# Regrouped loads, one fold for the attention biases, and a longer waking matmul in a three-layer attention kernel

## The chip, the cores and the metric

The kernel runs on one core of one Trainium2 chip. The metric is the device time in microseconds of one launch. The engines are TensorE (PE in the profile, with its weight loads as PEld), VectorE (DVE), ScalarE (ACT), GpSimd (POOL) and SyncE (SP), which in this kernel issues nearly all DMAs.

## The reference

A batch of 16 sequences of 256 tokens with 256 features (`x`), and a context `y` of the same size. All numbers are float32. There are 16 heads of 16 features.

```python
# layer 0: cross-attention with RMS norms
q, c = rmsnorm(x, g_q), rmsnorm(y, g_c)
x = rmsnorm(x + softmax((q @ Wq) (c @ Wk)^T / 4) (c @ Wv) @ Wo, g_out)
# layer 1: causal self-attention, with biases and rotary positions
h = ln1(x);  x = x + attn(rope(h @ sa_wq + b), rope(h @ sa_wk + b), h @ sa_wv + b, causal) @ sa_wo + b
# layer 2: cross-attention with the context
h = ln2(x);  x = x + attn(rope(h @ ca_wq + b), rope(y @ ca_wk + b), y @ ca_wv + b) @ ca_wo + b
# then an MLP
h = ln3(x);  out = x + gelu(h @ fc1_w + fc1_b) @ fc2_w + fc2_b
```

Each layer norm has a gain `g` and a bias `b`. The kernel never applies them to the tokens. It multiplies the gain into the rows of the weight that follows (`fold_gain`), and computes `b @ W` once with a few small matmuls, to add it to the bias of that product ("a fold").

## The kernel before, in words

The 48 attentions (3 layers x 16 batches) run one after the other in the order that the string `ORDER` gives (line 31): 0 is layer 0, 1 the causal self-attention, 2 the second cross-attention. One pass of the loop over `i` is called slot `i` here, and takes some 13 to 15 us. The first slots are of layers 0 0 0 0 0 1 0 1 0 1 0 2 2 1 0 2. The MLP of all batches follows, in seven-product form (`Mlp`), from 727 us on.

The order of instructions on each engine is written out by hand (`manual_schedule`): every engine takes its instructions in the order in which the Python calls are made. A slot has 4 steps `n` (3 in a causal slot). Each step issues the scores of one block (L484, PE), their exponentials (L495, ACT), in causal slots the mask (L502, POOL), and the product with the values of the step before (L523, PE); in between, PE works for the neighbours: `q`, `k` (L286) and `v` (L299) of attention i+1, the output projection (`project`, L299) of i-2, and the transpose of the normed tokens (`turn`, L266) of i+2.

An attention's result passes through DRAM. The copy of `av` out of PSUM (L540) is written to `hop` (L541). `end`, at step 0 of the next slot, writes the second half and reads back the softmax sums (`sums`, L548) and the rows (`oT`, L553). `invert`, at step 1, takes the reciprocal (L560), writes it to `inv_hop` (L562) and reads it back spread over the partitions (`inv`, L568). `divide` multiplies both (L574) a slot later. For layer 0, `send` and `receive` take the norm's factor the same way, through `rq_hop` (L363) to `rq` (L371).

Loads of inputs: each attention of layer 0 needs its batch's x and y in two layouts, rows (`x`, `y`) and transposed (`xT`, `yT`), 256 KB each. Batches 0 to 3 are loaded before the loop, batch 4 in slot 0. From slot 2 on, a slot whose attention i+3 is of layer 0 (a load slot: 3, 5, 7, 11 and so on, 11 of them) calls `load` at its start, ahead of all its other DMAs: xT, x, yT, y. The weights of the later layers (`pieces`: three of `ca`, `cao`, four of `fc1`, four of `fc2`, 256 KB each) are issued one each at the end of steps 1 and 2 of the slots after 3 in which attention i+3 is not of layer 0. All go through SP's queue, in which `hop`, `sums`, `oT`, `inv` and `rq` stand too.

Folds: `fold_v` (L207) adds the layer norm's share to V's bias row of self-attention, at slot 0, step 3, with PE products and a DVE addition that waits for `bias_sb`. `fold_bias` makes the products for Q and K in one row each and writes them to DRAM (`fold_hop`); `fold_back` (L186) reads them back as columns, in 4-byte pieces. For self-attention these are at slots 1 and 2, the addition (`fold_sa`, L195) at slot 3. For cross-attention they are at slot 6, step 3 (products) and slot 8, step 2, where the read (`fold_back`), `fold_gain` and the addition (`fold_ca`, L198) are called together. For fc1 they are at slot 11 and at slot 14, step 2, where read and addition (`fold_fc1`, L202) are again called together.

The start: two matmuls on a tile of zeros (`idle`, L878, of 512 and 256 columns) run while the first loads are under way. `stats` (L238) computes the sums of squares on DVE, POOL takes the power (L231, into `pad` and `r_o`), and `spread` (L350, PE) spreads the factor of the first two batches.

Of the kernel before, what the change touches and what calls it, by code (L numbers as in the profile page):

```python
# [12 lines left out]
ALU = mybir.AluOpType  # L13
# [32 lines left out]
def xattn_kernel(  # L46
# [27 lines left out]
    def ctile(shape, name, dtype=F32):  # L74
        return const.tile(shape, dtype, tag=name, name=name)
# [8 lines left out]
    def rows_of(b):  # L84
        return cur[:, NC * b : NC * b + NC, :]
# [3 lines left out]
    xTs = {}  # L89
    yTs = {}  # L90

    def load_x(b):
        xTs[b] = work.tile([P, KC, S], F32, tag="xT", name=f"xT{b}", bufs=3)
        nc.sync.dma_start(out=xTs[b], in_=xt[b].rearrange("(k p) s -> p k s", p=P))
        nc.sync.dma_start(out=rows_of(b), in_=x[b].rearrange("(c p) d -> p c d", p=P))

    def load_y(b):
        yTs[b] = work.tile([P, KC, S], F32, tag="yT", name=f"yT{b}", bufs=Y_LIVE)
        nc.sync.dma_start(out=yTs[b], in_=yt[b].rearrange("(k p) s -> p k s", p=P))
        ys[b] = work.tile([P, NC, D], F32, tag="y", name=f"y{b}", bufs=3)  # L100
        nc.sync.dma_start(out=ys[b], in_=y[b].rearrange("(c p) d -> p c d", p=P))

    def load(b):
        load_x(b)
        load_y(b)

    def load_w(t, aps, eng):
        at = 0
# [7 lines left out]
    nc.scalar.dma_start(out=vec, in_=vecs)  # L116
    w0_sb = ctile([P, KC, 3 * D], "w0")
    load_w(w0_sb[:, :, : 2 * D], w0[:2], nc.scalar)
    load_x(0)
    load_y(0)  # L120
    mask_u8 = ctile([P, B * NC], "mask_u8", U8)
    w0o_sb = ctile([P, KC, D], "w0o")
    sa_sb = ctile([P, KC, 3 * D], "sa")
# [27 lines left out]
    def dense_ps():  # L151
        return psD.tile([P, 512], F32, tag="d", name="d")
# [38 lines left out]

    qk_cols = vec[:, V_QK : V_QK + 8].rearrange("p (n t) -> p n t", t=KC)

    def fold_sa(cols):
        nc.vector.tensor_tensor(qk_bias[:, 0:2], cols[:, 0:2], qk_cols[:, 0:2], ALU.add)  # L195

    def fold_ca(cols):
        nc.vector.tensor_tensor(qk_bias[:, 2], cols[:, 0], qk_cols[:, 2], ALU.add)  # L198
        nc.vector.tensor_copy(qk_bias[:, 3], qk_cols[:, 3])

    def fold_fc1(cols):
        nc.vector.tensor_tensor(  # L202
            fb1.rearrange("p (j t) -> p j t", t=KC), cols,
            vec[:, V_FC1B : V_FC1B + FF // P].rearrange("p (j t) -> p j t", t=KC), ALU.add,
        )

    def fold_v():  # L207
        ps = dense_ps()
        for k in range(KC):
            for j in range(0, P, 32):  # L210
                nc.tensor.matmul(
                    ps[j : j + 32, :D],
                    lhsT=vec[:, V_B1 + k : V_B1 + k + 1].to_broadcast([P, 32]),
                    rhs=sa_sb[:, k, 2 * D : 3 * D],
                    start=(k == 0), stop=(k == KC - 1), skip_group_check=True,
                )
        row = bias_sb[:, R_SAV : R_SAV + D]
        nc.vector.tensor_tensor(row, ps[:, :D], row, ALU.add)

    def fold_gain(w, cols, vcol, chunks=range(KC), eng=nc.vector):  # L220
        for k in chunks:
# [652 lines left out]
    with tc.manual_schedule():  # L874

        idle = psS.tile([P, 2, 512], F32, tag="S", name="idle")[:, 0]
        for n in (512, 256):
            nc.tensor.matmul(idle[:, :n], lhsT=ident, rhs=zeros[:, :n], start=True, stop=True)  # L878
        fold_gain(w0_sb, slice(0, D), V_GQ)

# [23 lines left out]
        pieces = [(ca_sb[:, :, j * D : (j + 1) * D], [ca[j]], nc.sync) for j in range(3)]  # L904
        pieces.append((cao_sb, [ca_o], nc.sync))
        for j in range(4):
            cols = slice(j * D, (j + 1) * D)
            pieces.append((fc1_sb[:, :, cols], [fc1[:, cols]], nc.sync))
        for j in range(4):
            pieces.append((fc2_sb[:, 2 * j : 2 * j + 2], [fc2[j * D : (j + 1) * D]], nc.sync))  # L910
        for i in range(N_ATT):
            a, last = att(i), att(i - 1)
            ahead = att(i + 3)
            if i > 1 and ahead is not None and ahead.layer == 0:
                load(ahead.b)

# [7 lines left out]
            for n in range(len(a.blocks)):  # L924
                if n == 0 and a.causal and not finishing:
                    do(i + 2, "stats")
                a.scores(n)
                if n > 0:
                    a.values(n - 1)
                elif last is not None:  # L930
                    last.values(-1)
                final = len(a.blocks) - 1
                if n == 0:
                    if i == 0:
                        a.v()
# [12 lines left out]
                    if i == N_ATT - 3:  # L948
                        mlps[0].stats()
                    if i == N_ATT - 2:  # L950
                        mlps[0].norm()
                    do(i - 2, "divide")
                    if i == N_ATT - 1:
                        mlps[0].turn(nc.vector.tensor_copy)
                        mlps[0].keep()
                    do(i + 1, "q")
                elif n == 1:

                    if a.causal:
# [12 lines left out]
                    if i == N_ATT - 1:  # L972
                        do(i - 2, "project")
                        mlps[1].norm()
                if n == final - 1:
                    do(i + 1, "v")
                    if i == N_ATT - 2:
                        mlps[1].stats()
                    if i == N_ATT - 1:
                        mlps[0].up(2)  # L980
                        mlps[0].mix("hT")
                if n == final:
                    if i == N_ATT - 1:
# [530 lines left out]
```

## Time and profile before

| | |
|---|---|
| Median of 3 runs | 949.86 us (947.06, 949.86, 951.55) |
| Profiled execution, its own time | 948.64 us |
| Its span, first to last instruction | 946.9 us |
| Mean granted TensorE clock | 0.997 |
| DVE busy | 664.8 us (70%) |
| ACT busy | 547.0 us (58%) |
| POOL busy | 310.6 us (33%) |
| DMA, SP's queue | 80.58 MB, 27.0% of 16 engines' span |

PE is busy for nearly all of the span, so a mean says little here: it has to be asked where PE stands, and behind what. The view of windows gives PE's busy time in stretches of 20 us; the timeline of a short stretch shows each engine's instructions in order of time and, in brackets, how long the engine stood before one and what released it. The ends of matmuls are modelled, so a wait can hide in a busy PE: a group of matmuls that starts late after the one before is then seen only by comparing start times with those of the same group elsewhere.

Two landmarks for the timeline: slot 5 begins at 89.41, slot 6 at 103.50, slot 8 at 133.35, slot 9 at 148.91, slot 14 at 228.49 and slot 15 at 244.63 us.

### The profile page before, as it was taken

The numbers are of one execution on the slowest core, as the hardware profiler recorded it, in microseconds if no ns is written. First come the engines' busy times: TensorE is split into PE (matmuls) and PEld (weight loads), VectorE is DVE, ScalarE is ACT, GpSimd is POOL, SyncE is SP. The second block draws the span as 40 slices with busy tenths as digits, with TensorE's granted clock in tenths as the row PEclk, the third lists the DMA queues.
The fourth block names the chain that finished last, engine by engine and source line by source line (L and its number), as shares of the span: only waits on it lengthen the run. The fifth ranks groups of instructions, "written<-read, shape, count | busy, mean of one in ns | idle before, by whom it ended". The sixth has DMA issues, their size and how long they took to land.

```text
span 946.9 us, 29342 instructions
## 1 busy us (share of the span) xinstructions
PE 934.5 (99%) x12390; PEld 551.1 (58%) x12390; DVE 664.8 (70%) x1439; ACT 547.0 (58%) x773; POOL 310.6 (33%) x503
## 2 busy tenths in 40 slices
PE   8999998999999999999999999999999999999997
PEld 4444454445454555455455454555444799999997
DVE  4457765776777778768876677988877576676663
ACT  3666654765656665756656666666666634444440
POOL 4213452315352554434443333454133021222200
PEclk9999999999999999999999999999999999999999
DMA  9443343524242232322434221222222100000001
GB/s 293 139 118 107 110 157 86 165 70 145 64 128 87 73 125 87 115 78 71 126 110 133 87 90 62 80 68 71 77 72 81 46 23 24 12 12 24 23 24 47
DMA packets 99893, 83.07 MB, mean 88 GB/s; under 512 B 22686, under 2 KB 99498, under 8 KB 99754
## 3 DMA queue, kind: packets, MB, share of 16 engines
q1 hardware_dynamic: 99066, 80.58, 27.0%
q8 instruction: 99, 1.62, 0.7%
q10 hardware_dynamic: 688, 0.54, 0.2%
q14 instruction: 40, 0.33, 0.1%
HBM read 50.92 MB, written 30.17 MB: 86 GB/s over the span
## 4 chain that ended last, share of the span: by engine, by line
PE 91%; DMA 4%; DVE 2%; SPq 1%; issue 1%; POOL 0%; ACT 0%; ACTq 0%; DVEq 0%
PE S L484 18%; PE A L523 17%; PE d L286 16%; PE d L299 16%; PE upX L688 6%; PE A L786 5%; PE downZ L786 3%; PE upZ L688 3%; PE d L266 2%; PE d L786 2%; PE d L688 1%; DMA hop<-av 1%; DMA cols<-fold_hop 1%; PE d L664 1%; PE downX L786 1%
## 5 line engine op out<-in xcount | busy, mean ns | idle before, releaser
L495 ACT ACTIVATE pt<-S 128x1024 f32<-128x1024 f32 x224 | 217.3, 1022 | 119.9 <-PE S L484 119.7
L484 PE MATMUL S<-qm,kT 32*128 32x512 f32 (+1 forms) x1536 | 201.8, 600 | 0.0
L523 PE MATMUL A<-pt,va 128*32 128x256 f32 (+1 forms) x3072 | 190.4, 368 | 3.5 <-POOL pt L502 2.5
L523 PEld LDWEIGHTS A<-pt,va 128*32 128x32 f32 x3072 | 80.4, 109 | 157.9 <-issue 106.8
L495 ACT ACTIVATE pt<-S,sy 128x1024 f32<-128x1024 f32 x128 | 135.6, 1111 | 46.4 <-PE S L484 45.9
L502 POOL TENSOR_SCALAR_AFFINE_SELECT pt<-pt 128x512 f32<-128x512 f32 x128 | 88.8, 709 | 62.5 <-ACT pt L495 62.2
L484 PEld LDWEIGHTS S<-qm,kT 32*128 32x128 f32 x1536 | 62.3, 183 | 65.3 <-issue 41.2
L275 POOL TENSOR_TENSOR cur<-cur,bias 128x512 f32<-128x512 f32 x48 | 66.5, 1391 | 56.5 <-DVE xn L255 56.5
L230 POOL TENSOR_SCALAR r_ln<-bmv 128x2 f32<-128x2 f32 x48 | 14.1, 295 | 214.7 <-DVE bmv L249 213.5
L394 ACT ACTIVATE a<-d,qk_bias 128x256 f32<-128x256 f32 x128 | 53.6, 470 | 52.4 <-PE d L286 40.9
L286 PE MATMUL d<-hT,sa 128*32 128x256 f32 x1024 | 61.1, 379 | 0.0
L583 DVE TENSOR_TENSOR cur<-d,cur 128x512 f32<-128x512 f32 x32 | 22.0, 687 | 44.7 <-PE d L299 44.7
L255 DVE TENSOR_SCALAR xn<-cur,bmv,r_ln 128x256 f32<-128x256 f32 x96 | 52.1, 591 | 1.4 <-POOL r_ln L231 0.8
L540 DVE COPY av<-A 128x512 f32<-128x512 f32 x47 | 32.4, 688 | 26.6 <-PE A L523 25.6
L402 DVE TENSOR_TENSOR u<-u,turn 128x512 f32<-128x512 f32 x64 | 49.7, 777 | 0.0
L402 DVE TENSOR_TENSOR a<-a,turn 128x512 f32<-128x512 f32 x64 | 47.2, 737 | 2.2
L398 DVE STREAM_SHUFFLE u<-a 128x512 f32<-128x512 f32 x64 | 47.5, 742 | 0.0
L726 ACT ACTIVATE g<-g,fb 128x256 f32<-128x256 f32 x96 | 41.0, 499 | 11.1 <-DVE g L715 11.1
L230 POOL TENSOR_SCALAR r_o<-ms_o 128x2 f32<-128x2 f32 x16 | 3.8, 240 | 132.0 <-DVE sq L238 122.4
L286 PEld LDWEIGHTS d<-hT,sa 128*32 128x32 f32 x1024 | 33.5, 110 | 21.8
L574 DVE TENSOR_TENSOR oT<-oT,inv 128x512 f32<-128x512 f32 x48 | 42.6, 889 | 3.2 <-issue 2.5
L781 DVE TENSOR_TENSOR g<-g,g 128x512 f32<-128x512 f32 x64 | 40.9, 681 | 0.0
(152 smaller groups left out, 1572.1 us busy)
## 6 DMA issues: line engine op xcount, KB each, us to landing
hop<-av SPq DMA_DIRECT2D x96, 256.0 KB
oT<-hop SPq DMA_DIRECT2D x96, 128.0 KB
inv<-inv_hop SPq DMA_DIRECT2D x96, 128.0 KB
xT<-in_xt SPq DMA_DIRECT2D x16, 256.0 KB
cur<-in_x SPq DMA_DIRECT2D x16, 256.0 KB
yT<-in_yt SPq DMA_DIRECT2D x16, 256.0 KB
y<-in_y SPq DMA_DIRECT2D x16, 256.0 KB
out<-res SPq DMA_DIRECT2D x15, 256.0 KB
```

The lines of the kernel that those rows point to most:

```text
L255: nc.vector.tensor_scalar(xn[:, c, :], src[:, c, :], mv[:, c, 0:1], r[:, c : c + 1], ALU.subtract, ALU.mult,)
L275: nc.gpsimd.tensor_tensor(t, t, bias_sb[:, row : row + D].unsqueeze(1).to_broadcast([P, NC, D]), ALU.add)
L286: nc.tensor.matmul(ps[j : j + 32, t * S : (t + 1) * S], lhsT=w[:, k, at + t * P + j : at + t * P + j + 32], rhs=src[:, k, :], start=(k == ...
L299: nc.tensor.matmul(ps[j : j + 32, c * D : (c + 1) * D], lhsT=src[:, k, c * P + j : c * P + j + 32], rhs=w[:, k, at : at + D], start=(k == ...
L394: nc.scalar.activation(a[:, t], ps[:, t], AF.Identity, bias=bias[:, t : t + 1])
L402: nc.vector.tensor_tensor(t, t, table.unsqueeze(1).to_broadcast([P, KC, S]), ALU.mult)
L484: nc.tensor.matmul(ps[:, j, 2 * m * u : 2 * m * (u + 1)] .rearrange("p (i s) -> p i s", i=2), lhsT=self.kT[r, t, kc * P : (kc + 1) * P], r ...
L495: nc.scalar.activation(pt[:, :, :w], ps[:, :, :w], AF.Exp, scale=scale)
L502: nc.gpsimd.affine_select(out=diag, in_=diag, compare_op=ALU.is_ge, fill=0.0, base=0, pattern=[[0, 2], [0, 2], [1, P]], channel_multiplier=-1,
L523: nc.tensor.matmul(self.av[32 * r : 32 * r + 32, i, q0:S], lhsT=self.va[:, kc, 8 * t + 2 * r + i, :], rhs=pts[r // 2][:, r % 2, i * m : (i ...
L688: nc.tensor.matmul(banks[c // 2][:, (c % 2) * S : (c % 2 + 1) * S], lhsT=a[:, c * P : (c + 1) * P], rhs=b, start=(first and c % 2 == 0), s ...
L786: nc.tensor.matmul(ps[:, c, :], lhsT=a[f // 2][:, f % 2, c * P : (c + 1) * P], rhs=b[:, f, :], start=(first and c == 0 and f == 0), stop=True,
```

## The change

- Loads of the loop: `batch` makes the list of a batch's four loads, in the order x, y, xT, yT. In a load slot the four are put at the head of a list `due`, in which the later weights (without Wq of cross-attention) already wait. `load_next(i)` issues from the list at two places of a slot: at step 0 behind `end`, and at step 1 behind `invert` and `receive`. In a load slot it issues two each time, else one each time from slot 3 on.
- Before the loop and in slot 0, batches 1 to 4 are loaded in the order x, y, xT, yT; batch 0 keeps xT, x, yT, y.
- Wq of cross-attention is loaded at slot 0, step 1, instead of slot 4.
- Folds: one call at slot 1, step 3 makes the products for Q, K and V of self-attention and Q of cross-attention. Slot 2 reads the columns back, and the V row, spread over all partitions, into a new tile `row_v`. `fold_att` at slot 3, step 3 makes all additions. `fold_v`, the call of `fold_bias` at slot 6 and the addition at slot 8 are gone; `fold_gain` at slot 8 stays.
- fc1's fold is read back at slot 12, step 1, and added at slot 14, step 2 as before.
- The second waking matmul has 384 columns instead of 256.

```diff
+    def load(b, order=(0, 1, 2, 3)):
+        pieces = batch(b)
+        for n in order:
+            nc.sync.dma_start(out=pieces[n][0], in_=pieces[n][1])
...
-    load_x(0)
-    load_y(0)
+    load(0, (2, 0, 3, 1))
...
+    def fold_att(cols, row_v):
+        for n, j in ((0, 0), (1, 1), (2, 3)):
+            nc.vector.tensor_tensor(qk_bias[:, n], cols[:, j], qk_cols[:, n], ALU.add)
         nc.vector.tensor_copy(qk_bias[:, 3], qk_cols[:, 3])
+        row = bias_sb[:, R_SAV : R_SAV + D]
+        nc.vector.tensor_tensor(row, row_v, row, ALU.add)
...
-        for n in (512, 256):
+        for n in (512, 384):
...
+        def load_next(i):
+            n = 2 if i > 1 and ahead is not None and ahead.layer == 0 else int(i > 2)
+            for t, w in due[:n]:
+                nc.sync.dma_start(out=t, in_=w)
+            del due[:n]
+
         for i in range(N_ATT):
...
             if i > 1 and ahead is not None and ahead.layer == 0:
-                load(ahead.b)
+                due[:0] = batch(ahead.b)
...
                     do(i - 1, "end")
+                    load_next(i)
...
                     do(i + 2, "receive")
+                    load_next(i)
...
-                if i == 0 and n == 3:
-                    fold_v()
+                if i == 0 and n == 1:
+                    load_w(ca_sb, ca[:1], nc.sync)
...
-                    sa_hop = fold_bias([(sa_sb, 0, V_B1), (sa_sb, D, V_B1)] * 2)
+                    att_hop = fold_bias(
+                        [(sa_sb, j * D, V_B1) for j in range(3)] + [(ca_sb, 0, V_B2)]
+                    )
                 if i == 2 and n == 2:
-                    sa_cols = fold_back(sa_hop)
+                    att_cols = fold_back(att_hop)
+                    row_v = ctile([P, D], "row_v")
+                    nc.sync.dma_start(out=row_v, in_=att_hop[2].partition_broadcast(P))
...
                 if i == 3 and n == 3:
-                    fold_sa(sa_cols)
-                if i > 3 and n in (1, 2) and ahead is not None and ahead.layer > 0:
-                    for piece in pieces[:1]:
-                        load_w(*piece)
-                    del pieces[:1]
-                if i == 6 and n == 3:
-                    ca_hop = fold_bias([(ca_sb, 0, V_B2)] * 4)
+                    fold_att(att_cols, row_v)
                 if i == 8 and n == 2:
-                    ca_cols = fold_back(ca_hop)
                     fold_gain(ca_sb, slice(0, D), V_G2)
-                    fold_ca(ca_cols)
...
+                if i == 12 and n == 1:
+                    fc1_cols = fold_back(fc1_hop)
                 if i == 14 and n == 2:
-                    fold_fc1(fold_back(fc1_hop))
+                    fold_fc1(fc1_cols)
```

More of the change, by code (lines that the diff above doesn't have):

```diff
@@ L90, in xattn_kernel, with batch @@
     yTs = {}
-    def load_x(b):
+    def batch(b):
         xTs[b] = work.tile([P, KC, S], F32, tag="xT", name=f"xT{b}", bufs=3)
-        nc.sync.dma_start(out=xTs[b], in_=xt[b].rearrange("(k p) s -> p k s", p=P))
-        nc.sync.dma_start(out=rows_of(b), in_=x[b].rearrange("(c p) d -> p c d", p=P))
-    def load_y(b):
         yTs[b] = work.tile([P, KC, S], F32, tag="yT", name=f"yT{b}", bufs=Y_LIVE)
-        nc.sync.dma_start(out=yTs[b], in_=yt[b].rearrange("(k p) s -> p k s", p=P))
         ys[b] = work.tile([P, NC, D], F32, tag="y", name=f"y{b}", bufs=3)
[L101 to L105, printed above, removed]
+        return [
+            (rows_of(b), x[b].rearrange("(c p) d -> p c d", p=P)),
+            (ys[b], y[b].rearrange("(c p) d -> p c d", p=P)),
+            (xTs[b], xt[b].rearrange("(k p) s -> p k s", p=P)),
+            (yTs[b], yt[b].rearrange("(k p) s -> p k s", p=P)),
+        ]
+    def load(b, order=(0, 1, 2, 3)):
+        pieces = batch(b)
+        for n in order:
+            nc.sync.dma_start(out=pieces[n][0], in_=pieces[n][1])
     def load_w(t, aps, eng):
@@ L192, in xattn_kernel @@
     qk_cols = vec[:, V_QK : V_QK + 8].rearrange("p (n t) -> p n t", t=KC)
[L194 to L198, printed above, removed]
+    def fold_att(cols, row_v):
+        for n, j in ((0, 0), (1, 1), (2, 3)):
+            nc.vector.tensor_tensor(qk_bias[:, n], cols[:, j], qk_cols[:, n], ALU.add)
         nc.vector.tensor_copy(qk_bias[:, 3], qk_cols[:, 3])
+        row = bias_sb[:, R_SAV : R_SAV + D]
+        nc.vector.tensor_tensor(row, row_v, row, ALU.add)
     def fold_fc1(cols):
@@ L205, in fold_fc1 @@
         )
[L207 to L218, printed above, removed]
     def fold_gain(w, cols, vcol, chunks=range(KC), eng=nc.vector):
@@ L902, in xattn_kernel @@
             kept.setdefault(slot, []).append(j)
-        pieces = [(ca_sb[:, :, j * D : (j + 1) * D], [ca[j]], nc.sync) for j in range(3)]
-        pieces.append((cao_sb, [ca_o], nc.sync))
+        due = [(ca_sb[:, :, j * D : (j + 1) * D], ca[j]) for j in (1, 2)] + [(cao_sb, ca_o)]
         for j in range(4):
             cols = slice(j * D, (j + 1) * D)
-            pieces.append((fc1_sb[:, :, cols], [fc1[:, cols]], nc.sync))
+            due.append((fc1_sb[:, :, cols], fc1[:, cols]))
         for j in range(4):
-            pieces.append((fc2_sb[:, 2 * j : 2 * j + 2], [fc2[j * D : (j + 1) * D]], nc.sync))
+            due.append((fc2_sb[:, 2 * j : 2 * j + 2], fc2[j * D : (j + 1) * D]))
+        due = [(t, w.rearrange("(k p) n -> p k n", p=P)) for t, w in due]
+        def load_next(i):
[3 more added lines that the diff above has]
+            del due[:n]
         for i in range(N_ATT):
```

## The prediction

> **What bounds the kernel now.** I read the busy table first, then the windows of 20 us, the waits, and the timeline of each place where TensorE stood.
>
> ```profile
> PE 934.5 (99%) x12390; PEld 551.1 (58%) x12390; DVE 664.8 (70%) x1439; ACT 547.0 (58%) x773; POOL 310.6 (33%) x503
> ```
>
> TensorE (PE) is the bound: 934.5 of 946.9 us. Whatever leaves PE's busy time alone can win at most the 12.4 us in which PE stands, plus what PE does at half clock. In the windows of 20 us those lie in few places: 0 to 20 (16.80 busy), 100 to 120 (19.27), 140 to 160 (17.48), 240 to 260 (19.00) and the last 7 us; everywhere else PE shows 19.98 or more.
>
> ```profile
> 140.00:160.00 20.00, 17.48 (x244) 8.14 (x240) 12.78 (x32) 10.32 (x12) 5.10 (x10) 0.91 0.32 89
> ```
>
> The columns after the length are PE, weight loads, DVE, ACT, POOL, then the granted clock: 0.91 here. Of the waits, two are for a bias that returns from DRAM:
>
> ```profile
> DVE qk_bias L198 <- DMA cols<-fold_hop: 6.3, 1, 6.3
> DVE fb L202 <- DMA cols<-fold_hop: 5.6, 1, 5.6
> ```
>
> The first, in slot 8, step 2, in the timeline (start, length, what; in brackets the idle time before it):
>
> ```profile
> 147.49 0.56 SPq L186 DMA_DIRECT2D cols<-fold_hop  x1
> ...
> 152.71 1.15 PE L484 MATMUL S<-qm,kT 32*128 32x256 f32 x16
> 152.79 0.16 DVE L198 TENSOR_TENSOR qk_bias<-cols,vec 128x2 f32<-128x2 f32 x1 [6.26 <-DMA cols<-fold_hop]
> ...
> 154.65 0.22 POOL L230 TENSOR_SCALAR r_o<-ms_o 128x2 f32<-128x2 f32 x1 [15.78 <-DVE sq L238]
> ...
> 156.38 2.29 PE L523 MATMUL A<-pt,va 128*32 128x256 f32 x14 [2.52 <-POOL pt L502]
> ...
> 162.98 1.14 PE L484 MATMUL S<-qm,kT 32*128 32x512 f32 x8
> ```
>
> DVE stands 6.26 us for a load issued in the same step; POOL stands behind DVE's sums, the causal mask (L502) behind POOL, and PE behind the mask for 2.52 us. The second, in slot 14, step 2 (PE stands in slot 15):
>
> ```profile
> 248.43 1.14 PE L484 MATMUL S<-qm,kT 32*128 32x512 f32 x8
> ...
> 249.73 0.69 DVE L540 COPY av<-A 128x512 f32<-128x512 f32 x1
> ...
> 250.57 1.07 PE L523 MATMUL A<-pt,va 128*32 128x256 f32 x16 [1.00 <-DVE av L540]
> ```
>
> Slot 5 is a load slot with no fold in it:
>
> ```profile
> 93.21 1.15 PE L484 MATMUL S<-qm,kT 32*128 32x256 f32 x16
> ...
> 93.35 0.37 SPq L541 DMA_DIRECT2D hop<-av  x1
> ...
> 98.74 1.14 PE L484 MATMUL S<-qm,kT 32*128 32x512 f32 x8
> ...
> 99.10 0.55 SPq L548 DMA_DIRECT2D sums<-hop  x1
> ...
> 102.91 0.67 PE L266 MATMUL d<-ident,xn 128*128 128x128 f32 x4 [0.73 <-DVE xn L255]
> ```
>
> The write of `hop` takes 5.7 us (93.35 to 99.10), since a weight and the four loads of a batch, issued from 89.90 to 92.81, are ahead of it; DVE waits for `sums`, `xn` is late, PE stands 0.73. The start:
>
> ```profile
> 2.09 2.93 PE L878 MATMUL idle<-zeros,ident 128*128 128x512 f32 x4 [2.09 <-POOL zeros L160]
> ...
> 5.68 3.64 PE L286 MATMUL d<-xT,w 128*32 128x256 f32 x32 [0.67 <-DVE w L222]
> ...
> 9.88 1.90 PE L286 MATMUL d<-yT,w 128*32 128x256 f32 x32
> ```
>
> The same 32 matmuls take 3.64 us cold and 1.90 warm; PE stood 0.67 between the waking matmuls and the first real ones.
>
> [...] after the 2.52 us of idleness the clock is 0.50 from 157 to 159 and 1.00 again from 160. [...] at the start 0.67 us was too much, if the gap was the cause. [...]
>
> **The change part by part.**
>
> (1) Cross-attention's bias goes home with self-attention's: read back in slot 2, added in slot 3. DVE's wait of slot 8 is gone. Its price is read from the twin: from the 16 score matmuls to the next scores slot 5 needs 98.74 - 93.21 = 5.53 us, slot 9 needs 162.98 - 152.71 = 10.27. Same program, so 4.74 us (2.52 standing, the rest half clock). What is late next? In slot 5 nothing in that stretch; minus 4.74.
>
> (2) The fc1 bias is fetched at slot 12 and used at slot 14: two slots of some 15 us for a load that took under 6. PE then needs 1.07 for the scores instead of 250.57 - 248.43 = 2.14: minus 1.07. The fetch (SP 0.46 us, 1024 small pieces) stands ahead of the first `hop` write of slot 12, which is read only a slot later: 0.
>
> (3) The separate fold of slot 6 goes (16 passes at 119.20, 0.86 us in the chain). PE was dense on both sides and a projection of 1.73 stays in that step, so ACT (two exponentials, 2.12) is done before the next scores: minus 0.86, its ACT copy (0.37) and SP issue with it. The fold of slot 1 keeps its size: two repeated columns become V of self-attention and Q of cross-attention.
>
> (4) `fold_v` goes (16 passes, 0.86). Its step in slot 0 has no projection: scores end at 26.2, the two exponentials run to 28.41, and the scores after them end 1.1 later, at 29.5, with or without it. So 0 (bound: 0.86). DVE loses a 2.63 us wait for `bias` that hid nothing. If its cover, ACT, were gone, the 0.86 would come back.
>
> (5) Added at slot 3, step 3: three additions at 0.08 us start to start, the copy, and a 256-wide addition (0.42, as L218 took): 0.74 in place of 0.08. DVE stood 1.01 us right there (75.47 to 76.48), which hides it; uncovered it would cost 0.66. `row_v` (128 KB) is loaded in slot 2, 15 us ahead; behind it on SP is the write of `hop`, about 0.9 us in all (issue 0.5, rings 0.4) against a slot: 0.
>
> (6) Loads. At slot start went 4 issues (about 0.5 us each on SP) ahead of `hop`. Now two follow `oT<-hop` and two follow the inversion and `receive`. `hop` is back at 3.5 us, so `sums` comes 2.2 earlier than 101.09: minus 0.73 in slot 5. In return x and y stand ahead of `inv_hop` on SP and in the rings: 2 x 0.5 plus 2 x 0.93 (256 KB at the 282 GB/s of the first window) = at most 2.9 us. The divide that needs `inv` comes at 293.21, the last `inv` issue ended at 288.30: 4.9 us of slack in such a slot, 0. After slot 12 no slot with a batch also sends `rq`. The weights go the same way, one per place: half of that. Wq of cross-attention moves to slot 0 behind `receive`, ahead of two `hop` writes: 0.93 us, against 3.43 us for which DVE stands at 39.99 afterwards: 0.
>
> (7) The start. The order x, y, xT, yT brings y of batch 2 two loads sooner (DVE waited 0.58 for it at 17.40) and xT of batch 1 two later, about 12.8 instead of 10.9 by the landings, needed at 15.62: 0. The second waking matmul grows by half: 2.93 us were 1536 columns, 256 more (two passes of 128) are 0.49, so the gap shrinks from 0.67 to 0.18 and nothing is delayed. [...] the first 32 matmuls end up to 1.73 us earlier; `rq` cannot come before the `pad` of 7.97 and DVE is busy with y to 9.14, while `qm` began at 10.54: at most 1.4. [...] Between 0 and 1.4 (a loss would need the waking to outlast 5.68) I take 0.7.
>
> Sum: 4.74 + 1.07 + 0.86 + 0.73 + 0.7 = 8.1. The profiled execution took 948.64 (span 946.9 and 1.7 around it), so 940.5. It lies 1.2 under the median of the runs, 949.86, from which the same sum gives 941.8. I forecast 941.0.
>
> **Rivals.** R1: the waking always works: 1.4 instead of 0.7, about 940. For it: cold 3.64 against 1.90. [...] R2: the stalls are partly replaced. Behind DVE's wait POOL or the causal mask is nearly as late, so half of parts 1 to 3 comes back: 0.5 x 6.67 = 3.3, giving 944.3. For it: DVE ran without a break from 152.8 to 159.3. Against: slot 5, and the dense steady state after 260. R3, slower: x and y ahead of `inv_hop` make `inv` late in every slot with a batch, DVE's divide waits in order, and PE behind it. From 4.9 us on it decides. My 2.9 leaves 2; if it were 6.2, PE would lose 1.3 in each of the 11 slots, 14.3 - 8.1 = 6.2 more than before: 954.8 against the profiled time, about 955. Against: `inv_hop<-sums` is 16 KB[...]. R4: the waking does nothing and the rest holds: 941.2 to 942.
>
> **How the numbers follow.** Forecast with R4: 0.52, own range 939.5 to 943. R1: 0.14. R2: 0.26, reaching to 947, a little under half of it above 945.1. R3: 0.08. A measurement of this kernel tells about 0.5% from no change, 945.1 to 954.6. Faster 0.52 + 0.14 + 0.14 = 0.80; same 0.12 and a little of R3, 0.13; slower 0.07. The range runs from 938 (all gains, 1.4 at the start, part of `fold_v`) to 946.5, which leaves R3 and the end of R2 out.
>
> **What would show it.** Right: no DVE wait on `cols`; PE over 19.8 in the windows that hold slots 5, 9 and 15, clock 1.00 there; 5.5 us for slot 9's stretch; `hop` under 4 us in load slots. Wrong: new brackets of PE behind DVE `oT` (L574's successor) or behind `inv`, or the first 32 matmuls at 3.64 again, which takes the start's 0.7 away.

## The result, and the profile after

The changed kernel took 940.9 us (median of 6 runs, 940.26 to 941.61) against 949.64 us for the kernel before on the same chip (6 runs, 947.06 to 951.55). The ratio is 0.9913, with a 95% interval of 0.9896 to 0.9930. The forecast was 941.0. The profiled execution took 940.73 us and has a span of 939.0, 7.9 less than that of the kernel before, at a mean granted clock of 0.999 (0.997 before).

The busy table of the kernel after (engine, busy time, share of the span, instructions):

```profile
PE 929.7 (99%) x12358; PEld 548.6 (58%) x12358; DVE 662.7 (71%) x1440; ACT 547.1 (58%) x772; POOL 311.4 (33%) x503
```

TensorE has 4.8 us less of busy time, of which the 32 removed passes of the two folds are only some 1.7. Most of the rest was never work: a group of matmuls that stood, or ran at half clock, counts as busy (14 of slot 9's late value products show as 2.29 us before, all 16 as 1.07 now). So the windows come next (start:end, length, then the busy time of PE, PEld, DVE, ACT and POOL with the number of instructions, the granted clock, the DMA share and GB/s). These are the stretches of the kernel after that hold slots 5 and 6, slot 9 and slot 15:

```profile
100.00:120.00 20.00, 20.00 (x307) 9.71 (x300) 15.37 (x38) 14.05 (x18) 7.71 (x13) 1.00 0.41 127
140.00:160.00 20.00, 20.00 (x320) 10.32 (x316) 13.31 (x33) 11.79 (x14) 8.00 (x14) 1.00 0.36 107
240.00:260.00 20.00, 20.00 (x312) 9.87 (x308) 16.22 (x29) 12.81 (x17) 10.95 (x14) 1.00 0.27 83
```

PE is busy for all of them, at a granted clock of 1.00. Before they had 19.27, 17.48 and 19.00 us, and the middle one a clock of 0.91 with 244 matmuls where 320 now fit.

A wait that is inside a group of matmuls shows only against the same group elsewhere, so I lined up the start times of the same value products (`A<-pt`) in both traces. Their difference stays constant except at six places:

| Place | start before | start after | step there | step predicted |
|---|---|---|---|---|
| Start and slot 0 | 18.53 | 18.10 | -0.43 | -0.7 |
| Slot 5 | 104.57 | 103.33 | -0.81 | -0.73 |
| Slot 6, the separate fold | 121.07 | 118.96 | -0.86 | -0.86 |
| Slot 9, first value product | 156.38 | 151.68 | -2.59 | together -4.74 |
| Slot 9, the next one | 164.05 | 157.21 | -2.15 | |
| Slot 15 | 250.57 | 242.66 | -1.07 | -1.07 |
| From there to the end | | | 0 | 0 |

The steps add up to 7.91, which is the change of the span. Slot 9 in the timeline of the kernel after:

```profile
149.64 1.49 POOL L490 TENSOR_SCALAR_AFFINE_SELECT pt<-pt 128x512 f32<-128x512 f32 x2
...
150.61 1.15 PE L472 MATMUL S<-qm,kT 32*128 32x256 f32 x16
...
151.68 1.07 PE L511 MATMUL A<-pt,va 128*32 128x256 f32 x16
...
156.14 1.14 PE L472 MATMUL S<-qm,kT 32*128 32x512 f32 x8
```

The mask (POOL) begins a microsecond before the scores of the next block and is in time; all 16 value products run at once. From 150.61 to 156.14 are 5.53 us, the figure that the twin in slot 5 gave. In slot 5 the timeline after reads:

```profile
92.43 0.36 SPq L529 DMA_DIRECT2D hop<-av  x1
...
95.63 0.55 SPq L536 DMA_DIRECT2D sums<-hop  x1
...
97.73 0.18 DVE L547 TENSOR_SCALAR sums<-sums 128x32 f32<-128x32 f32 x1 [2.24 <-DMA sums<-hop]
...
101.68 0.66 PE L254 MATMUL d<-ident,xn 128*128 128x128 f32 x4
```

From the write of `hop` to the issue of the read behind it are 3.2 us instead of 5.7; over all 11 load slots this is now 2.2 to 3.9 us, where it was 2.9 to 5.8. In some of the slots behind them, where xT and yT now stand ahead of `hop`, it is longer than before: 4.9 us in slot 6, before 2.7. DVE still stands 2.24 us for `sums`, but the transposes of `xn` have no bracket any more: PE doesn't stand. In slots 14 and 15:

```profile
234.59 0.16 DVE L203 TENSOR_TENSOR fb<-cols,vec 128x8 f32<-128x8 f32 x1
...
241.59 1.14 PE L472 MATMUL S<-qm,kT 32*128 32x512 f32 x8
242.66 1.07 PE L511 MATMUL A<-pt,va 128*32 128x256 f32 x16
```

The addition for fc1 has no wait in front of it (the read was issued at 205.76), and from the scores to the values PE needs 1.07. The start:

```profile
2.09 3.25 PE L866 MATMUL idle<-zeros,ident 128*128 128x512 f32 x4 [2.09 <-POOL zeros L161]
5.44 1.93 PE L274 MATMUL d<-xT,w 128*32 128x256 f32 x32
...
9.48 1.65 DVE L422 SCALAR_TENSOR_TENSOR qm<-d,vec,rq 128x256 f32<-128x256 f32 x4
...
10.89 0.99 POOL L882 MEMSET va<- 128x512 f32 x2
11.05 1.24 DVE L210 TENSOR_SCALAR w<-w,vec 128x256 f32<-128x256 f32 x2
...
14.73 0.64 PE L338 MATMUL A<-ident,pad 128*32 128x128 f32 x16 [0.66 <-POOL pad L219]
```

The waking worked: the first 32 matmuls take 1.93 us instead of 3.64, and `qm` begins at 9.48 instead of 10.54. Of these 1.06 us only 0.43 reach the spread of the second batch (14.73, before 15.16). DVE's scaling of the next weight takes 1.24 us where it took 0.61: it now lies beside POOL's memset of `va`, which it followed before. The start also varies from one execution to the next; what these 0.43 us stand for is taken up with the waking experiments.

One wait grew, in the view of waits of the kernel after (total, times, longest):

```profile
DVE oT L562 <- DMA inv<-inv_hop: 5.8, 4, 2.7
```

Before, the same line summed to 0.6. The longest is in slot 22, where DVE stood in the kernel before too; there the profile names no transfer as the cause:

```profile
354.20 1.64 DVE L574 TENSOR_TENSOR oT<-oT,inv 128x512 f32<-128x512 f32 x1 [1.76 <-issue]
```

So at this divide the wait grew from 1.76 to 2.71 us. No more than 0.1 us is lost there, but the timeline of the kernel after shows that there is no reserve:

```profile
347.23 0.70 DVE L562 TENSOR_TENSOR oT<-oT,inv 128x512 f32<-128x512 f32 x1 [2.71 <-DMA inv<-inv_hop]
...
355.35 0.69 DVE L431 TENSOR_TENSOR kT<-a,u 128x512 f32<-128x512 f32 x1
...
356.19 1.14 PE L472 MATMUL S<-qm,kT 32*128 32x512 f32 x8
```

Behind the divide DVE works without a break up to `kT`, which it ends at 356.04. The scores that read `kT` begin 0.15 us later. The change did not use up a reserve here: in the kernel before, where the divide itself took 1.64 us instead of 0.70, `kT` ended at 363.94, 0.14 us ahead of the scores at 364.08.

### The profile page after: what moved, and what is told of

It is laid out like the page before. It is cut to its first block, busy times and chain, and to the rows that moved or that the text cites. A ratio compares the mean times of both kernels' runs of the same rounds, so it can differ in the third digit from the quotient of the medians.

```text
span 939.0 us, 29252 instructions
## 1 busy us (share of the span) xinstructions
PE 929.7 (99%) x12358; PEld 548.6 (58%) x12358; DVE 662.7 (71%) x1440; ACT 547.1 (58%) x772; POOL 311.4 (33%) x503
## 4 chain that ended last, share of the span: by engine, by line
PE 98%; DMA 1%; DVE 0%; SPq 0%; POOL 0%; issue 0%; ACT 0%; DVEq 0%
PE S L472 20%; PE A L511 19%; PE d L287 17%; PE d L274 17%; PE upX L676 6%; PE A L774 5%; PE downZ L774 3%; PE upZ L676 3%; PE d L254 2%; PE d L774 2%; PE d L676 1%; PE d L652 1%; PE downX L774 1%; DMA y<-in_y 1%; PE d L172 0%; SPq L107 0%
## 5 line engine op out<-in xcount | busy, mean ns | idle before, releaser
L562 DVE TENSOR_TENSOR oT<-oT,inv 128x512 f32<-128x512 f32 x48 | 39.6, 824 | 5.8 <-DMA inv<-inv_hop 5.8
```

## The experiments

The theory: each gain lies at one place, and is the stall that the trace of before shows there; the folds give the most, and the loads and the waking little. The rivals are those of the prediction: the stalls are partly replaced by the next late thing, `inv` becomes late behind x and y, the waking does nothing.

**The attention folds alone.** The kernel before, with Q of cross-attention folded in slot 1 and all additions in slot 3; its old load order stays.

```diff
-                if i == 0 and n == 3:
-                    fold_v()
+                if i == 0 and n == 1:
+                    load_w(ca_sb, ca[:1], nc.sync)
...
-                    sa_hop = fold_bias([(sa_sb, 0, V_B1), (sa_sb, D, V_B1)] * 2)
+                    att_hop = fold_bias(
+                        [(sa_sb, j * D, V_B1) for j in range(3)] + [(ca_sb, 0, V_B2)]
+                    )
...
-                if i == 6 and n == 3:
-                    ca_hop = fold_bias([(ca_sb, 0, V_B2)] * 4)
...
-                    ca_cols = fold_back(ca_hop)
...
-                    fold_ca(ca_cols)
```

> The kernel before with only the attention folds changed (one fold at slot 1, Wq of cross-attention loaded in slot 0, no fold_v, no fold at slot 6, no read at slot 8). My theory: slot 6 starts its successor 0.86 us earlier, the 10.27 us of slot 9 become 5.53, nothing at slots 5 and 15, and nothing from fold_v in slot 0: 5.6 us less than the kernel before, about 944. Rival, stall replaced: behind DVE's wait something else is nearly as late in slot 9, half of the 4.74 comes back and 3.2 us are gained.

Measured: 944.82 us (943.59 to 946.59), ratio 0.9926 (0.9900 to 0.9951). By start times slot 6 gives 0.86, slot 9 gives 2.59 and 2.15, each to the hundredth what the whole change gives there. So these two belong to the folds alone, and R2 is wrong for them. But the profiled execution is the longest of the four, and slot 5 in its timeline says why:

```profile
93.22 0.41 SPq L541 DMA_DIRECT2D hop<-av  x1
...
100.15 0.55 SPq L548 DMA_DIRECT2D sums<-hop  x1
...
103.23 0.18 DVE L559 TENSOR_SCALAR sums<-sums 128x32 f32<-128x32 f32 x1 [7.64 <-DMA sums<-hop]
...
104.18 0.67 PE L266 MATMUL d<-ident,xn 128*128 128x128 f32 x4 [2.34 <-DVE xn L255]
```

With the old load order `hop` took 6.9 us here, PE stood 2.34 instead of 0.73, and the clock fell to half from 105.14 to 108.56 (0.91 over 100 to 120): 3.24 us lost against the kernel before. The stall that the regrouped loads remove is not always 0.73; it differs from one execution to the next, and is called a draw from here on.

**The read of fc1's fold alone,** at slot 12 in the kernel before.

```diff
+                if i == 12 and n == 1:
+                    fc1_cols = fold_back(fc1_hop)
                 if i == 14 and n == 2:
-                    fold_fc1(fold_back(fc1_hop))
+                    fold_fc1(fc1_cols)
```

> The kernel before with fc1's fold read back at slot 12 instead of slot 14. My theory: PE's 1.00 us of standing in slot 15 goes, 1.07 us less in the profile, all else as before. Rival: the 1024 small pieces of the read delay the hop write of slot 12, and a stall there takes the place of the one in slot 15: 0.

Measured: 948.28 us (946.88 to 951.27), ratio 0.9975 (0.9962 to 0.9987). Slot 15 gives 1.07 by start times, as in the whole change. The rest of the profiled difference lies at places that the edit doesn't touch: the start -0.77, slot 5 +0.51, slot 9 +0.81. The kernel before draws these anew in each execution. The medians lie 1.9 us apart, which is more than the 1.07; the one trace doesn't show what the rest is.

**The loads alone:** `batch` and `load_next` in the kernel before, with Wq of cross-attention at the head of `due` and the folds where they were.

```diff
             if i > 1 and ahead is not None and ahead.layer == 0:
-                load(ahead.b)
+                due[:0] = batch(ahead.b)
...
                     do(i - 1, "end")
+                    load_next(i)
...
                     do(i + 2, "receive")
+                    load_next(i)
...
-                if i > 3 and n in (1, 2) and ahead is not None and ahead.layer > 0:
...
```

> The kernel before with only the loads regrouped (two places of a slot, x and y first), all folds as before. My theory: hop comes back in under 4 us in slot 5, PE's 0.73 us there goes (0.81 by start times), the stalls of slots 9 and 15 stay: about 0.8 us less. Rival: x and y ahead of inv_hop make the divide late in the 11 load slots: 5 us more or worse.

Measured: 952.19 us (950.86 to 954.86), ratio 1.0015 (1.0002 to 1.0028). My expectation failed. Slot 5 gives 0.81, as said; slot 9 loses 1.28 and 0.88, and slot 15 loses 2.23 and 1.69. The timeline around slot 14, step 2, shows what happened:

```profile
243.75 0.46 SPq L916 DMA_DIRECT2D xT<-in_xt  x1
244.26 0.47 SPq L916 DMA_DIRECT2D yT<-in_yt  x1
...
245.29 0.47 SPq L187 DMA_DIRECT2D cols<-fold_hop  x1
...
250.13 0.17 DVE L203 TENSOR_TENSOR fb<-cols,vec 128x8 f32<-128x8 f32 x1 [8.05 <-DMA cols<-fold_hop]
...
253.40 1.76 PE L524 MATMUL A<-pt,va 128*32 128x256 f32 x16 [3.23 <-DVE av L541]
```

In slot 14 the new order puts xT and yT right ahead of the read of `cols`. Before, it was issued at 243.44 and DVE had it at 247.31, 3.87 us later; now it is issued 1.85 us later in the trace (1.25 counted from the scores before it) and takes 4.84. DVE waits 8.05 us instead of 5.56, PE stands 3.23 instead of 1.00, and the granted clock over 240 to 260 is now 0.91, where it was 1.00. Slot 8 is another matter: only one weight is ahead of that read, where there were two, and it is issued 0.96 us sooner, but DVE has it only 0.28 us sooner (152.51), since it takes 6.0 us instead of 5.3. PE had come 1.56 us sooner to the scores ahead of it; that gain runs into the wait, PE stands 3.80 us instead of 2.52, and half clock lasts 6.8 us, where before it lasted 3.41 (156.57 to 159.98). In the whole change neither can happen, since no fold is read in the step that needs it. So the parts don't add up: alone, the new load order makes the kernel slower by 0.15%, and beside the early reads it gives what was forecast.

**Half clock or standing in slot 9?** Two extra matmuls of 512 columns ahead of the late value product of the kernel before, into a bank that nothing reads, so that PE isn't idle there.

```diff
                 a.scores(n)
+                if i == 9 and n == 1:
+                    warm = dense_ps()
+                    for _ in range(2):
+                        nc.tensor.matmul(warm, lhsT=ident, rhs=w0_sb[:, 0, :512], start=True, stop=True)
```

> The kernel before with two more matmuls of 512 columns on PE in slot 9, behind the scores of step 1, where PE then stands for 2.52 us; their output is read by nobody. My theory: of the 4.74 us that slot 9 loses, 2.52 are standing and 2.2 are the half clock after it. Two matmuls of 0.86 fill 1.7 us of the standing, the clock stays at 1.00 and the stretch from the 16 scores to the next scores falls from 10.27 to about 8.1. Rival: the 2.2 us are DVE and POOL catching up, the clock has nothing to do with it: 10.27 stays.

Measured: 949.84 us (947.45 to 953.42), ratio 0.9994 (0.9980 to 1.0008): not resolved as a time. The timeline answers:

```profile
151.86 1.15 PE L484 MATMUL S<-qm,kT 32*128 32x256 f32 x16
...
152.93 1.98 PE L931 MATMUL d<-w,ident 128*128 128x512 f32 x4
...
155.71 0.63 PE L523 MATMUL A<-pt,va 128*32 128x256 f32 x4 [0.80 <-POOL pt L502]
156.51 0.84 PE L523 MATMUL A<-pt,va 128*32 128x256 f32 x10 [0.17 <-POOL pt L502]
...
160.95 1.14 PE L484 MATMUL S<-qm,kT 32*128 32x512 f32 x8
```

The granted clock is 1.00 over 140 to 160, and the stretch shrinks from 10.27 to 9.09 us, not to the 8.1 that I had expected. So half clock was 1.2 of the 4.74 (1.4 if the stretch is counted from the late value product, which came 0.18 later after its scores here), and standing some 3.5: the bracket of 2.52, and the rest within the product, which waits once more for the second mask. The prediction had put only the bracket down to standing.

Why was this execution not faster as a whole? It lost 4.83 us at a place where the trace of the kernel before shows nothing, at the end of load slot 29:

```profile
468.05 1.35 PE L484 MATMUL S<-qm,kT 32*128 32x512 f32 x8 [3.14 <-DVE kT L443]
```

DVE had waited 4.09 us for `sums`, whose `hop` is issued behind the four loads of that slot and took 6.55 us, `kT` was late, and the clock fell to half for 3.41 us. By start times this place cost 0, 0, 0.4, 0.85 and 4.83 us in the five executions with the old load order, and nothing in the eight with the new one (the kernel with eight extra copies, below, left aside). The regrouped loads remove this draw too; the prediction had no term for it.

**The waking alone:** in the kernel before with 384 columns, and in the kernel after with 256.

```diff
-        for n in (512, 256):
+        for n in (512, 384):
```

> The kernel before with the second waking matmul at 384 columns and nothing else changed. My theory: the gap ahead of the first real matmuls shrinks from 0.67 to about 0.2 us, [...] the first scores come up to 1.1 us earlier, about 0.4 of it is left in slot 1: 0.4 us less, stalls of slots 5, 9 and 15 as before. Rival: [...] the clock comes as late as before, and nothing is gained.

> The kernel after with the second waking matmul back at 256 columns. My theory: the full clock comes at up to 10 us [...]; 0.4 us more than the kernel after if so[...]; never more than 1.1. The rest of the gain, 7.5 us, stays. Rival: the waking is what the whole start hangs on, and 1.4 us or more are lost.

Measured: 949.01 us (945.28 to 952.02) for the first, ratio 0.9992 (0.9979 to 1.0006), and 942.49 us (941.50 to 942.85) for the second, ratio 0.9919 (0.9894 to 0.9943), against 949.39 of the kernel before. In the kernel before, the time can't tell the waking from nothing. In the kernel after it can: 942.49 stands against 940.33 (940.11 to 940.74) for the next kernel below, which adds only hidden work to the kernel after and ran on the same chip. This is more than the 1.1 us that I had set as the most; the rival of that expectation, 1.4 or more, came nearer. The traces show where it lies. With 384 columns, in the kernel before:

```profile
2.09 3.35 PE L878 MATMUL idle<-zeros,ident 128*128 128x512 f32 x4 [2.09 <-POOL zeros L160]
5.40 2.48 PE L286 MATMUL d<-xT,w 128*32 128x256 f32 x32
```

With 256 columns, in the kernel after:

```profile
6.25 3.64 PE L274 MATMUL d<-xT,w 128*32 128x256 f32 x32 [1.24 <-DVE w L210]
```

The gap was 1.24 us, since the weight came later in that execution; the 32 matmuls took 3.64 us again, the 16 behind them 1.08 instead of 0.64 and the next 32 2.09 instead of 1.93, and the start is 1.11 us later than with 384 columns; slot 22 adds 0.97, with PE standing 1.00 for `kT`. Over all traces of this study, the first 32 matmuls took 1.93 to 3.17 us in the eight starts with 384 columns; of the six with 256, three took 3.64 and three 2.59 to 3.20. After gaps of 0.67, 0.99 and 1.24 us it was 3.64, but with 384 columns a gap of 0.51 gave 1.93 (`fold_v` put back) and one of 0.20 gave 3.17 (three extra copies): the gap alone doesn't settle it. Nor does the granted clock show the slower pace: from 5 to 9 us it reads 1.00 in the trace of the kernel before, with 3.64, as in that of the kernel after, with 1.93. Fast first matmuls aren't all of the start, though: the value product that begins at 18.53 in the trace of the kernel before and at 18.10 in that of the kernel after begins at 17.15 to 17.78 in three other kernels with 256 columns (fc1's fold, the loads and the extra matmuls of slot 9 alone), and at 17.75 to 18.48 in the four with 384 columns that edit the kernel after without moving the memset. So the 0.43 us are the difference of two draws, and not the size of the waking.

**`fold_v` again:** its 16 passes put back into the kernel after, with a result that nothing reads.

```diff
+                if i == 0 and n == 3:
+                    extra = dense_ps()
+                    for k in range(KC):
+                        for j in range(0, P, 32):
+                            nc.tensor.matmul(
+                                extra[j : j + 32, :D],
+                                lhsT=vec[:, V_B1 + k : V_B1 + k + 1].to_broadcast([P, 32]),
...
```

> The kernel after with the 16 passes of the old fold_v put back on PE at slot 0, step 3; their result is read by nobody. My theory: ACT's two exponentials end the step there, so the 0.86 us of PE work are hidden and slot 1 begins as in the kernel after: 0. Rival: PE's order decides, 0.86 us more.

Measured: 940.33 us (940.11 to 940.74), ratio 0.9902 (0.9865 to 0.9939). The timeline of slot 0 with the passes, and then that of the kernel after without them:

```profile
26.52 1.05 PE L995 MATMUL d<-sa,vec 128*32 128x256 f32 x16
27.50 1.60 PE L472 MATMUL S<-qm,kT 32*128 32x512 f32 x8
28.76 2.12 ACT L483 ACTIVATE pt<-S,sy 128x1024 f32<-128x1024 f32 x2 [0.84 <-PE S L472]
29.03 1.07 PE L511 MATMUL A<-pt,va 128*32 128x256 f32 x16
```

```profile
27.03 2.13 PE L472 MATMUL S<-qm,kT 32*128 32x512 f32 x8 [0.26 <-ACT pt L483]
28.29 2.12 ACT L483 ACTIVATE pt<-S,sy 128x1024 f32<-128x1024 f32 x2 [0.30 <-PE S L472]
29.09 1.07 PE L511 MATMUL A<-pt,va 128*32 128x256 f32 x16
```

The scores begin 0.47 us sooner without the passes and then take 2.13 instead of 1.60, since half of them wait for ACT. The value product begins at the same time. ACT hides `fold_v`, and its removal is worth nothing.

**How near is R3?** Copies of 256 KB from DRAM to DRAM, which nothing reads, ahead of `inv_hop` in each load slot of the kernel after: 3 in the first kernel, 8 in the second.

```diff
                     load_next(i)
+                    if i > 1 and ahead is not None and ahead.layer == 0:
+                        for e in range(3):
+                            nc.sync.dma_start(out=spare[e], in_=x[e])
```

> The kernel after with three more copies of 256 KB (DRAM to DRAM, read by nobody) behind x and y in each of the 11 load slots, ahead of inv_hop on SP and in the rings. My theory: each delays inv by 0.5 to 0.93 us, 1.5 to 2.8 together; of the 4.9 us of slack about 2.7 were used in the kernel after, so the divide begins to wait but PE loses at most 0.6 a slot, 0 to 6 us in all. Rival (R3 of the prediction, earlier than priced): the divide is already at the edge, PE loses 1.5 to 2.8 in each of 11 slots, 16 to 30 us.

> The same with eight more copies in each load slot. My theory: inv comes 4 to 7.4 us later, past the slack: PE stands for 2 to 5 us in each load slot and falls to half clock behind it, 20 to 70 us more. Rival: the slack is far larger than the 4.9 us that I read from the divide, since its result is needed only by the projection at the end of the slot: under 5 us more.

Measured: 946.35 us (942.40 to 948.52), ratio 0.9962 (0.9946 to 0.9978), with 3; 981.38 us (980.18 to 982.17), ratio 1.0331 (1.0306 to 1.0356), with 8. Against the 940.9 of the kernel after that is some 5.4 and 40.5 us, on average 0.5 and 3.7 for each of the 11 load slots; in the traces it is spread unevenly (with 8 copies slot 6 alone loses 7.7). Two lines of the waits view with 8 copies:

```profile
DVE oT L565 <- DMA inv<-inv_hop: 37.1, 12, 5.6
...
PE S L475 <- DVE kT L434: 28.9, 11, 5.4
```

and slot 6, behind load slot 5, in the timeline (for the divide the profile names no transfer that it waited for):

```profile
118.28 0.69 DVE L565 TENSOR_TENSOR oT<-oT,inv 128x512 f32<-128x512 f32 x1 [9.34 <-issue]
...
126.40 2.09 PE L475 MATMUL S<-qm,kT 32*128 32x512 f32 x8 [5.45 <-DVE kT L434]
```

The mechanism of R3 is real: with 8 copies queued ahead of `inv_hop`, DVE's divide waits (9.34 us in slot 6), `kT` behind it on DVE is late, and PE stands behind both (5.45 us there). It decides only some way beyond what the change puts there; 3 more copies are already too many.

**What holds the rest?** Three tries at a better kernel, from the two costs that the change left behind. First the memset of `va`, moved ahead of the norm of the first batch, so that it doesn't lie beside DVE's scaling:

```diff
+        for va in vas:
+            nc.gpsimd.memset(va[:, :, :, HD:], 1.0)
...
-        for va in vas:
-            nc.gpsimd.memset(va[:, :, :, HD:], 1.0)
```

> The kernel after with POOL's two memsets of va (0.99 us at 10.89, beside which DVE's scaling of Wv took 1.24 us instead of 0.62) moved ahead of the first norm, where POOL stood for 4.61 us. My theory: the scaling takes 0.62 again, DVE's chain to the second norm comes 0.6 us earlier, slot 1 about 0.5: 0.5 us less than the kernel after. Rival: the longer scaling is a wait for Wv in disguise, or ACT's exponentials set the step: 0.

Measured: 941.31 us (940.87 to 942.75), ratio 0.9917 (0.9889 to 0.9944). The scaling takes 0.61 again, and the start is 1.18 us earlier than in the kernel after, more than I had expected; slot 22 gives 1.58 back. There, in the timeline:

```profile
344.89 0.92 SPq L529 DMA_DIRECT2D hop<-av  x2
...
347.81 1.38 DVE L562 TENSOR_TENSOR oT<-oT,inv 128x512 f32<-128x512 f32 x1 [4.49 <-DMA yT<-in_yt]
...
351.06 0.55 SPq L536 DMA_DIRECT2D sums<-hop  x1
...
353.29 0.35 DVE L548 RECIPROCAL sums<-sums 128x32 f32<-128x32 f32 x1 [0.45 <-DMA sums<-hop]
...
356.59 1.14 PE L472 MATMUL S<-qm,kT 32*128 32x512 f32 x8 [1.60 <-DVE kT L431]
```

The divide waits 4.49 us instead of 2.71 (the profile puts this down to yT, which the divide doesn't read; it reads `inv`), and DVE waits once more for `sums`, whose `hop` is issued right behind xT and yT and takes 6.2 us from issue to the read (5.1 in the kernel after, 3.9 before). So `kT` is late and PE stands 1.60. Then x and y one slot earlier, to take them from ahead of `inv_hop`; and both edits together:

```diff
+            after = att(i + 4)
+            if n == 1 and i > 1 and after is not None and after.layer == 0:
+                loads = loads + batch_rows(after.b)
...
```

> The kernel after with x and y of a batch loaded one slot earlier, behind receive, so that no input is ahead of inv_hop in a load slot; weights as in the kernel after. My theory: in slot 22 DVE stood 2.7 to 4.5 us for inv and PE 0 to 1.6 us behind it, in one execution more than in another; DVE's wait there falls to 1.8 us or less, as in the kernel before, and PE does not stand. In the profile 0 against the kernel after, whose execution lost nothing there; in the median of the runs 0 to 0.5 less. Rival: the three loads that now end the slot before a load slot are ahead of the next hop write, DVE waits for sums, and a stall like that of slot 5 comes back: 0.7 us or more.

> The same, with the two memsets of va ahead of the first norm as in e10. My theory: slot 1 begins 1.2 us earlier than in the kernel after, as e10 showed, and slot 22 no longer gives it back: span about 937.8, median 939.5 to 940. Rival: what the start wins is lost at the next stage that was just in time, as in e10 (there 1.58 us in slot 22): 941.

Measured: 941.78 us (941.22 to 942.50), ratio 0.9921 (0.9902 to 0.9939), and 941.72 us (941.46 to 942.23), ratio 0.9920 (0.9902 to 0.9939), both against 949.57. With x and y gone from there, DVE still waits 2.78 us in slot 22, so my idea that they cause this wait is wrong; and here too DVE waits for `sums` (0.72), and PE behind it for `kT` (0.85). In the combined kernel the start wins 1.26, which slot 7 (1.32) and slot 22 (1.26) more than take back. In slot 7 DVE waits 4.54 us for `sums` and PE 1.24 behind it, the rival of the first expectation; in slot 22 the divide waits 4.16 us, `sums` is in time, and PE still stands 1.28. None of the three beats the change.

## Why the prediction was right, point by point

- (1) Slot 9: 4.74 forecast, 4.74 measured, in the whole change and with the folds alone. The total from the twin slot was right; its split was not. Half clock is 1.2 us of it, where the prediction's "2.52 standing, the rest half clock" implies 2.2. And the 15.78 us of POOL were not the size of the delay: POOL stands 11.90 us at the same place in the kernel after, where DVE waits for no bias.
- (2) and (3): 1.07 and 0.86, both exact and each found where it was said, (2) also by itself. The early reads wait for nobody: 0 as said.
- (4) `fold_v`: 0, with ACT as the cover, confirmed by putting the passes back.
- (5) The additions in slot 3 are hidden: the steps of the start times show nothing there.
- (6) Slot 5: 0.81 for 0.73, because a bracket of 0.73 isn't the whole delay; and slot 29, which had no term. What the prediction did not say is that this part depends on (1) and (2): alone it costs 0.15%. The 3.5 us to which `hop` was to return was misread: it is that of slot 14 (3.53 us), which is a load slot as well, with its four loads issued right ahead of that write (228.55 to 231.34). So what stands ahead in the queue isn't all that sets these times. That x and y cost nothing ahead of `inv_hop` was right, but the 4.9 us of slack was read from one slot (17) and counted from the end of the issue. In slot 22 DVE begins the divide only 2.6 us after that end, in the kernel before as in the one after, so about 2.3 would have been the better figure (an estimate: 4.9 less 2.6). The price set against it, 0.93 us for each load besides its issue, was an estimate too, from the 282 GB/s of the first window; that `inv` waits so long behind a load was not shown. Nor had the prediction priced xT and yT ahead of slot 22's `hop`: counted from the slot's first scores, `sums` is read 3.1 us later than before (10.3 against 7.25). In the kernel after both are just in time; in four of the experiments `sums` was 0.45 to 1.06 us too late there and PE stood 0.85 to 1.60, whether the start was earlier, the same or later.
- (7) The waking: 0.43 for 0.7 in these two traces, the largest miss of a single term. As the experiments show, these 0.43 are the difference of two draws, and the medians of the kernel after with 384 and with 256 columns lie 1.6 to 2.2 us apart, in part because of slot 22; so this term was not confirmed, and that the sum holds with it is in part luck. That a shorter gap makes the first matmuls fast was the author's estimate. The prediction's upper bound took for granted that DVE's next scaling would last as long as before; it moved beside POOL's memset and took 0.63 more.

Of the rivals, R1 (the waking always works) holds in this execution, where the first 32 matmuls took 1.93 us. Its worth isn't settled: the two traces differ by 0.43, the medians with 384 and 256 columns by more than its 1.4. R2 is wrong: nothing of slots 6, 9 and 15 was lost to a next late thing. R3 did not occur in the kernel after. Its chain (`inv`, the divide, `kT`, PE) has no reserve in slot 22, but x and y are not what makes `inv` late there. R4 is wrong by the kernel after with 256 columns. The sum by profile was 8.1 against 7.91. The medians differ by more, 8.7 us; that the forecast of 941.0 lies 0.1 from the measured 940.9 is luck too, since it lies between a sum from the profile (940.5) and one from the median (941.8). The kernel before scatters over 945.99 to 954.15 us in 43 runs, and the four slowest of them alone have a granted clock as low as 0.994; the kernel after scatters over 1.35 us in 6 runs, at 0.999 or 1.0. This fits stalls that bring half clock in some executions and not in others, as slot 5 with the folds alone and slot 29 showed (3.4 us each), and that the change removes. What each of them adds to the median isn't shown. Half clock followed on standing of 2.34 us (slot 5 with the folds alone) and of 2.52 us (slot 9 before); after 1.00 us (slot 15 before) the granted clock stayed at 1.00, and after 1.60 us (ahead of slot 23 with the memset moved) the next three groups took 1.14, 1.07 and 1.91 us, as elsewhere at 1.00.

What stays open: why DVE begins the divide of slot 22 2.7 us after the end of the issue of `inv` in the kernel after, 2.6 in the kernel before and 4.0 in the one with the memset moved; whether xT and yT behind that slot's `hop` would let the earlier start through, which the traces suggest and which wasn't tried; and, for the waking, what makes the first 32 matmuls take 1.93 us in one start and up to 3.64 in another.

## What to carry to other kernels

Price a stall from a twin of the stretch that doesn't have it, start to start, not from the idle bracket: this takes in the standing inside the groups and the half clock after it (4.74 us in slot 9, whose bracket was 2.52). When loads are regrouped, look for every small read that is issued in the step that needs it: here fc1's, with two loads put right ahead of it, took 4.84 us instead of 3.87, and in slot 8 a start 1.56 us sooner was lost in such a wait; move such reads a slot ahead first. And where a start is made earlier, ask at each engine what now lies beside it: in this kernel the two versions with an earlier start (by 1.18 and 1.26 us) lost all of it again further on, in slots without a reserve, one of which (22) had none in the kernel before either.

## What the runs showed that I had not expected

- The read of fc1's fold, 1024 pieces of 4 bytes, took 3.87 us from issue to use in the kernel before, and 4.84 right behind two loads of 256 KB; that of cross-attention's fold took 5.3 behind two weights and 6.0 behind one, so what is ahead in the queue isn't all of it.
- The scaling of two 128x256 float32 tiles on DVE took 1.24 us beside POOL's memset of 128x512, and 0.61 or 0.62 without it.
- Half clock lasted 3.41 us in slot 9 before, after 2.52 us of standing, and 3.42 in slot 5 with the folds alone, after 2.34. It cost 1.2 us in slot 9; with a stall of 3.80 us in slot 9 of the kernel with the loads alone it lasted 6.8 us.
